# The last row's layernorm, router and slots inside the second layer; its shared expert behind the experts; value sums on VectorE, the keys' maxima through TensorE

## The chip, the cores and the metric

One Trainium2 chip, one of its cores. The metric is device time of one execution in microseconds, and for a kernel the median of its runs. TensorE, VectorE (DVE), ScalarE (ACT), GpSimd (POOL) and the sync engine (SP, which issues most DMAs) each run a stream of instructions of their own, in the order of that stream, and wait for one another by semaphores.

## The reference

Two layers over x of 4 rows x 1024 tokens x 128 channels, in float32. Each layer normalises x and adds two branches of it to x.

```python
xn = _layernorm(x)
x = x + _L0_attn_ref(xn, ...) + _L0_ffn_ref(xn, ...)
xn = _layernorm(x)
x = x + _L1_attn_ref(xn, ...) + _L1_ffn_ref(xn, ...)
```

The first layer is an attention with 16 heads of 8 channels that share keys and values, beside an attention with 8 heads whose values and outputs go through 2 of 8 experts. The second layer, where the change lies, is this, much shortened:

```python
# L1 attention: positive random features, H=16 heads, J=64 features
dash = einsum('bhnd,hjd->bhnj', d**-0.25 * data, proj)
diag = sum(data * data) * 0.5 * d**-0.5
stab_q = max(dash, axis=-1); stab_k = max(dash, axis=(-1, -2))   # per head, over all tokens
feat = J**-0.5 * exp(dash - diag - stab) + EPS_FEAT
out = q' (k'^T v) / max(q' . sum(k'), EPS_DEN)
# L1 ffn: top 2 of 8 experts, and one shared expert for every token
top_w, top_i = top_k(xn @ gate_w + gate_b, 2); gw = softmax(top_w)
out = sum_e combine[:, e] * (gelu(xn @ w1[e] + b1[e]) @ w2[e] + b2[e])
shared = gelu(xn @ ws1 + bs1) @ ws2 + bs2
```

So the keys of a row need the greatest feature of each head over all 1024 tokens, and the constant EPS_FEAT needs the sum of the values over all tokens.

## The kernel before

x stays in SBUF, 128 tokens on the partitions, 8 tiles a row. The first layer is one long loop over units (row, head) with the other attention paced into it. When a row is complete, mqa_out (the last step of its attention) runs layernorm(1, b), which leaves the transposed row xnT[b] by TensorE, and router(b): the logits, the two best experts, by two products with constant matrices (L300) the place of each token in its expert's list, the shares, and at_slot. slot_rows(b) is then a generator of 16 steps; each normalises a tile of 128 tokens on GpSimd (L333), adds token number and share, and scatters it with an indirect DMA into sorted_x in HBM (L340). For rows 0 to 2 that lies within the first layer. Row 3 is complete only with the first layer's last product, so its norm and router stand at the layer's end, before the second layer.

The second layer begins with the loads of its weights (L1185 to L1225) into a pool fw, whose memory is that of the first layer's pools: the first of these is pre (gates and slots), the second wst (weights). Then the tables of blocks (L1236 to L1280): from how many tokens each expert has, which expert and which 256 slots each of 39 blocks takes (block, read by SP) and its bias (b1s).

Two orders are written by hand here, those of TensorE and SP; VectorE's and ScalarE's are planned ahead by the compiler from estimated times. GpSimd's instructions stand in the trace in the order of the program. The order comes from generators, of which each `yield` ends a step:

- favor_keys(b), 19 steps: project keys (kp), project values (v1p, va), diagonals (dg), project queries (qp), the sums of the values (vsum, L1363: 2 x 8 products with a column of ones), then four rounds of features (ddk, L1303): VectorE takes each token's maximum (mk, L1377) and subtracts it (L1313), ScalarE takes the exponential. Then mx is the maximum over the tiles, GpSimd's partition_all_reduce (L1386) makes of it stab, the maximum over all tokens, and VectorE scales va by exp(mk - dg - stab). Three steps later come the products kv (L1408).
- favor_queries(b), 20 steps: ask (ddq and exponentials) four times, turn (qt, 16 transposes) four times, outputs (fo), normalise (ot), turn_back (oT1p) and add (o1w, then x += by VectorE) twice.
- shared(), the shared expert: 8 tiles t of 512 tokens (two a row); ph and Gelu in one step, cT, py and bias in the next, the transposes back (yT) and the addition to x in the one after.
- experts(): for block j load sorted slots and w1, then turn (xgT), load w2, one (pb, Gelu), two (pe, VectorE's scaling yb, and two indirect DMAs with addition into the sums in HBM by GpSimd, L1673).

The fill, shared() and behind it the rest of the slots and experts(), goes between the others by a rate per step: 0.84 beside favor_keys(0) alone, 0.45 beside queries and keys together, 1.2 beside the last queries. In each of these steps the slots of row 3 take one step too. When all is issued, the sums are read back (y, L1738), added to x tile by tile (L1742) and stored (L1744).

The E tiles hold the exponentials, 2048 floats a partition, seven buffers in turn; in layernorm xn lies in cTs tiles, in shared() hT is a tile of its own. all_ones, ident and the PSUM banks (small) are shared by all.

Of the kernel before, what the change touches and what calls it, by code (L numbers as in the profile page):

```python
# [71 lines left out]
def two_layers(ctx: ExitStack, tc: tile.TileContext, a: dict, out: bass.AP):  # L72
# [141 lines left out]
    def layernorm(layer, b, pool):  # L214
# [12 lines left out]
        for q in range(NT // 4):  # L227
            xn = pool.tile([P, 512], F32, tag="cTs", name=f"xn{layer}_{b}_{q}", bufs=3)
# [119 lines left out]
    with ExitStack() as l0:  # L348
        pre = l0.enter_context(tc.tile_pool(name="pre0", bufs=1))
        wst = l0.enter_context(tc.tile_pool(name="wst", bufs=2))  # L350
# [348 lines left out]
        def mqa_out(b):  # L699
# [27 lines left out]

            if b == 0:
                nc.sync.dma_start(gw, a["gate_w"])
                nc.sync.dma_start(gb, a["gate_b"].unsqueeze(0).to_broadcast([P, ME]))  # L730
            while b not in complete:
                yield
# [498 lines left out]
    def brief(k, n, m, name):  # L1231
# [4 lines left out]
    nb = late([P, ME], "nb")  # L1236
    nc.vector.tensor_tensor(nb, filled, begin, ALU.subtract)
    nc.vector.tensor_scalar(nb, nb, 1.0 / MB, None, ALU.mult)
    more = brief(0, ME, PER, "more")
    nc.vector.tensor_tensor(  # L1240
        more, bcast(nb, PER), num[:, 0:PER].unsqueeze(1).to_broadcast([P, ME, PER]), ALU.is_gt
    )
    nc.vector.tensor_reduce(nb, more, axis=AX.X, op=ALU.add)
    upto = late([P, ME], "upto")
    nc.vector.tensor_copy(upto, nb)
    for e in range(1, ME):
        nc.vector.tensor_tensor(
            upto[:, e : e + 1], upto[:, e : e + 1], upto[:, e - 1 : e], ALU.add
        )

    past = brief(0, NBLK, ME, "past")
    full = [P, NBLK, ME]
    nc.vector.tensor_tensor(
        past, bcast(num[:, 0:NBLK], ME), upto.unsqueeze(1).to_broadcast(full), ALU.is_ge
    )
    of = late([P, 2, NBLK], "of")
    nc.vector.tensor_reduce(of[:, 0, :], past, axis=AX.X, op=ALU.add)
    nc.vector.tensor_tensor(past, past, nb.unsqueeze(1).to_broadcast(full), ALU.mult)
    nc.vector.tensor_reduce(of[:, 1, :], past, axis=AX.X, op=ALU.add)
    nc.vector.tensor_tensor(of[:, 1, :], num[:, 0:NBLK], of[:, 1, :], ALU.subtract)  # L1260
    nc.vector.scalar_tensor_tensor(
        of[:, 1, :], of[:, 0, :], float(PER), of[:, 1, :], ALU.mult, ALU.add
    )
    nc.vector.tensor_scalar(of[:, 1, :], of[:, 1, :], float(ME * PER), None, ALU.min)
    nc.vector.tensor_scalar(of[:, 0, :], of[:, 0, :], float(ME - 1), None, ALU.min)
    block = fw.tile([P, 2, NBLK], I32, tag="block", name="block")
    nc.vector.tensor_copy(block, of)

    b1s = late([P, NBLK, MHC], "b1s")
    isit = brief(0, NBLK, ME, "isit")  # L1270
    b1t = brief(1, NBLK, ME, "b1t")
    full = [P, NBLK, ME]
    nc.vector.tensor_tensor(
        isit, bcast(of[:, 0, :], ME), num[:, 0:ME].unsqueeze(1).to_broadcast(full), ALU.is_equal
    )
    for c in range(MHC):
        nc.vector.tensor_tensor(
            b1t, isit, b1[:, 0:ME, c].unsqueeze(1).to_broadcast(full), ALU.mult
        )
        nc.vector.tensor_reduce(b1s[:, :, c], b1t, axis=AX.X, op=ALU.add)  # L1280
# [41 lines left out]
    def favor_keys(b):  # L1322
# [6 lines left out]
        for q in range(2):  # L1329
# [7 lines left out]
            for c in range(2):  # L1337
                for r in range(2):
                    nc.vector.tensor_tensor(
                        va[:, ts(q, 4), c, :, 9 * r : 9 * r + HD], pv[:, :, :, c, r, :],  # L1340
                        bv[:, :, c, r, :].unsqueeze(1).to_broadcast([P, 4, 4, HD]), ALU.add,
                    )
        yield
# [17 lines left out]
        for c in range(2):  # L1361
            for n in range(NT):
                nc.tensor.matmul(  # L1363
                    vsum[:, c : c + 1], lhsT=va[:, n, c].rearrange("p s d -> p (s d)"),
                    rhs=ones[:, 0:1], start=(n == 0), stop=(n == NT - 1),
                )
# [7 lines left out]
        for r in range(NT // 2):  # L1374
# [10 lines left out]
        stab = fa.tile([P, 4, 4], F32, tag="stab", name=f"stab{b}")  # L1385
        nc.gpsimd.partition_all_reduce(  # L1386
            stab.rearrange("p s h -> p (s h)"), mx.rearrange("p s h -> p (s h)"), P,
            bass_isa.ReduceOp.max,
        )
        nc.vector.tensor_tensor(mk, mk, dg[:, 0], ALU.subtract)  # L1390
        nc.vector.tensor_tensor(
            mk, mk, stab.unsqueeze(1).to_broadcast([P, NT, 4, 4]), ALU.subtract
# [7 lines left out]
        yield  # L1400
# [162 lines left out]
    def shared():  # L1563
# [31 lines left out]
        for t in range(B * T // TC + 1):  # L1595
            if t < B * T // TC:
                b, q = divmod(t, T // TC)
                hT = hTs[t] = ff.tile([P, MHC, TC], F32, tag="hT", name=f"hT{t}", bufs=1)
# [7 lines left out]
            if t > 0:  # L1606
                third(t - 1)
            yield
            if t < B * T // TC:
# [93 lines left out]

    def fill():
        yield from shared()
        for it in to_slots.values():
            for _ in it:
                pass
        yield from experts()

    filler = fill()
    due = 0.0
    for k, (rows_now, rate) in enumerate((
        ((0,), 0.84), ((0, 1), 0.45), ((1, 2), 0.45), ((2, 3), 0.45), ((3,), 1.2),
# [3 lines left out]
        for _ in run(*its):  # L1718
            for it in to_slots.values():
                next(it, None)  # L1720
# [85 lines left out]
```

## Time and profile before

| what | us |
|---|---|
| median of 3 runs (lowest, highest) | 3413.81 (3403.72, 3414.24) |
| the profiled execution | 3414.98 |
| its span, first to last instruction | 3413.2 |
| TensorE busy, of the span | 3194.2 (94%) |
| VectorE, ScalarE, GpSimd busy | 2436.3, 1809.7, 1865.8 |
| granted TensorE clock, mean | 0.964 |
| last products of the first layer start | 2887.68 |
| first product of the second layer's own (kp) | 2912.60 |
| first product of the experts (xgT) | 3027.74 |
| last product | 3380.6 |

A line of the timeline gives start and length in us, engine, line and operation, what it writes and reads, how many are merged, and in brackets how long the engine stood before it and what ended that. TensorE's records of one kind follow each other faster than each lasts, since they are pipelined: the distance of their starts is what one costs. A float32 product has two records. A line of the waits gives who waited for whom, us in total, times, and the longest. "issue" in place of a releaser is time in which the profile shows nothing waited for. The granted clock is a share of full speed.

### The profile page before, as it was taken

The page shows a single profiled execution, that of the slowest core. Times are in us where ns is not written, and L with a number is a line of the kernel's source. Part 1 is how long each engine was busy: PE and PEld are TensorE (multiplying, and loading weights), DVE is VectorE, ACT ScalarE, POOL GpSimd, SP SyncE. Part 2 cuts the span into 40 slices and gives each one's busy share as a digit, 9 for nine tenths or more (in the row PEclk, how much of TensorE's full clock was granted, in tenths as well). Part 3 has the DMA queues.
Part 4 walks back from the last instruction along what each step waited for, and adds up shares of the span by engine and source line. Part 5 has one row for each costly group of instructions (what it writes and reads, how often), then busy time and mean ns, then how long its engine had stood idle before and what let it go on. Part 6 is the DMA issues. An engine that isn't in the chain of part 4 may idle for free. (4 is left out here: it accounts for less than half of the span.)

```text
span 3413.2 us, 48756 instructions
## 1 busy us (share of the span) xinstructions
PE 3194.2 (94%) x15386; PEld 1742.3 (51%) x15386; DVE 2436.3 (71%) x4714; ACT 1809.7 (53%) x3157; POOL 1865.8 (55%) x2355
## 2 busy tenths in 40 slices
PE   5899999999999999999999999999999998998996
PEld 2344444555545444554454445455455554567775
DVE  7998686766777867676877876777666645556774
ACT  2234555556555555655455555565566564345663
POOL 1345355666656666665467667656766553313334
PEclk8999999999999999999999999999999999888998
DMA  4122443432323223323232233232323220023346
GB/s 134 52 64 84 126 132 105 118 104 86 93 73 99 72 77 90 96 89 89 62 91 84 83 93 94 89 92 84 96 88 88 79 65 8 19 51 75 79 89 149
DMA packets 449335, 293.67 MB, mean 86 GB/s; under 512 B 41450, under 2 KB 422260, under 8 KB 449076
## 3 DMA queue, kind: packets, MB, share of 16 engines
q1 hardware_dynamic: 404884, 221.32, 23.0%
q0 software_dynamic: 41952, 68.16, 7.3%
q8 instruction: 123, 2.02, 0.2%
q14 instruction: 136, 1.11, 0.1%
q10 hardware_dynamic: 2240, 1.07, 0.1%
HBM read 176.29 MB, written 113.71 MB: 85 GB/s over the span
## 5 line engine op out<-in xcount | busy, mean ns | idle before, releaser
L618 DVE TENSOR_REDUCE nmh<-mx 128x1 f32<-128x512 f32 x1024 | 664.8, 682 | 278.0 <-PE mx L612 276.4
L860 POOL DMA_INDIRECT sorted_v<-xv,gates x448 | 446.7, 997 | 395.0 <-DMA sorted_v<-xv,gates 329.9
L673 ACT ACTIVATE pT<-sT 128x512 f32<-128x512 f32 x1024 | 557.2, 600 | 166.6 <-PE sT L666 97.7
L936 PE MATMUL ss<-xnT,qTs 128*128 128x512 f32 x1024 | 495.8, 606 | 7.2 <-DVE g_o L993 2.6
L941 DVE TENSOR_REDUCE nms<-ps 128x1 f32<-128x1024 f32 x256 | 311.1, 1215 | 256.0 <-ACT ps L939 254.9
L968 PE MATMUL cp<-pTs,vs 128*128 128x512 f32 x1024 | 460.9, 603 | 19.7 <-DVE pTs L960 16.5
L989 PE MATMUL po<-ow,cTs 128*128 128x512 f32 x1024 | 474.3, 595 | 0.7 <-ACT cTs L973 0.7
L821 POOL TENSOR_TENSOR g_o<-g_o 128x256 f32<-128x256 f32 x256 | 192.0, 750 | 465.2 <-DVE g_o L820 434.1
L939 ACT COPY ps<-ss 128x512 f32<-128x512 f32 x512 | 299.9, 587 | 256.1 <-PE ss L936 253.5
L943 ACT ACTIVATE ps<-ps,nms 128x1024 f32<-128x1024 f32 x256 | 294.4, 1150 | 156.1 <-DVE nms L941 155.2
L993 DVE TENSOR_TENSOR g_o<-po,go 128x512 f32<-128x512 f32 x512 | 334.2, 684 | 48.9 <-POOL x L999 26.9
L612 PE MATMUL mx<-ks,qs 72*128 72x512 bf16 x1024 | 312.3, 382 | 12.2 <-DVE nmh L618 5.1
L666 PE MATMUL sT<-qs,ks 75*128 75x512 bf16 x1024 | 310.3, 383 | 13.2 <-DVE nmh L618 9.3
L968 PEld LDWEIGHTS cp<-pTs,vs 128*128 128x128 f32 x1024 | 193.1, 194 | 246.1 <-issue 231.0
L936 PEld LDWEIGHTS ss<-xnT,qTs 128*128 128x128 f32 x1024 | 191.1, 193 | 188.9 <-issue 107.2
L956 PE MATMUL pTp<-ident,ps 128*128 128x128 f32 x2048 | 272.1, 276 | 13.9 <-ACT ps L943 10.4
L956 PEld LDWEIGHTS pTp<-ident,ps 128*128 128x128 f32 x2048 | 241.2, 142 | 81.2 <-issue 16.1
L989 PEld LDWEIGHTS po<-ow,cTs 128*128 128x128 f32 x1024 | 179.4, 191 | 159.1 <-issue 127.1
L973 ACT COPY cTs<-cp 128x512 f32<-128x512 f32 x64 | 37.5, 586 | 411.7 <-PE cp L968 411.7
L912 POOL DMA_INDIRECT vs<-yv,gates x224 | 219.0, 978 | 67.2 <-issue 56.6
L912 POOL DMA_INDIRECT yg<-yv,gates x224 | 217.6, 972 | 68.3 <-issue 68.0
L1673 POOL DMA_INDIRECT sum<-yb,whose x78 | 123.9, 1588 | 235.3 <-DVE yb L1669 199.1
(308 smaller groups left out, 4992.9 us busy)
## 6 DMA issues: line engine op xcount, KB each, us to landing
vb<-in_v_w_dram SPq DMA_DIRECT2D x644, 64.0 KB
xs<-sorted_v SPq DMA_DIRECT2D x140, 256.0 KB
yv<-xs SPq DMA_DIRECT2D x140, 256.0 KB
w<-in_w_dram SPq DMA_DIRECT2D x78, 256.0 KB
sorted_x<-nobody SPq DMA_DIRECT2D x16, 1040.0 KB
ow<-in_o_w_dram SPq DMA_DIRECT2D x32, 512.0 KB
qs<-qd SPq DMA_DIRECT2D x144, 64.0 KB
sorted_v<-xv,gates POOLq DMA_INDIRECT x448
```

What stands on the lines that cost most here:

```text
L612: nc.tensor.matmul(sc, lhsT=qs[0:NPAIR, i, ts(n, P)], rhs=ks[0:NPAIR, ts(kc, 512)], start=True, stop=True,)
L618: nc.vector.tensor_reduce(halves[:, i, n, kc : kc + 1], sc, axis=AX.X, op=ALU.max)
L666: nc.tensor.matmul(sc, lhsT=ks[:, ts(kt, P)], rhs=qs[:, i, ts(c, 512)], start=True, stop=True,)
L673: nc.scalar.activation(pT, sc, AF.Exp)
L860: nc.gpsimd.indirect_dma_start(out=sorted_v[u % 4][:, :], out_offset=bass.IndirectOffsetOnAxis(ap=column(u, k, n).bitcast(I32), axis=0), i ...
L912: nc.gpsimd.indirect_dma_start(out=to[:, n, :], out_offset=None, in_=unit[u, "y"][:, :], in_offset=bass.IndirectOffsetOnAxis(ap=column(u, ...
L936: nc.tensor.matmul(sc, lhsT=qT[:, ts(n, P)], rhs=xnT[b][:, ts(c, 512)], start=True, stop=True)
L941: nc.vector.tensor_reduce(nm, p, axis=AX.X, op=ALU.max, negate=True)
L956: nc.tensor.transpose(pt[:, ts(k, P)], p[:, ts(4 * k4 + k, P)], ident)
L968: nc.tensor.matmul(cp, lhsT=v[:, kt, :], rhs=pT[:, kt, :], start=(kt == 0), stop=(kt == NT - 1),)
L989: nc.tensor.matmul(po, lhsT=cT[:, ts(qt, P)], rhs=unit[u, "ow"][:, ts(c, 512)], start=True, stop=True,)
L993: nc.vector.tensor_tensor(g[:, ts(c, 4), :], po.rearrange("p (e c) -> p e c", e=4), bcast(go[:, ts(c, 4)], P), ALU.mult,)
```

## The change

1. mqa_out no longer norms and routes row 3. A generator last_row does it inside the second layer: layernorm with xn in E tiles, router, the tables of blocks (now the generator tables, same instructions), then the row's 16 slots. It takes two steps after each step of the loop.
2. shared() takes a range of tiles. Tiles 0 to 5 come first, then the experts, then tiles 6 and 7, which are row 3's, with hT in E tiles.
3. The sums of the values over a row's 8 tiles are made by one VectorE reduce into vs; TensorE keeps 2 products of 16.
4. The keys' maxima: mx is transposed by TensorE, reduced by VectorE, set on a diagonal (each) and sent to all partitions by a product with all_ones. favor_keys has 20 steps.
5. The rates beside queries and keys are 0.5 in place of 0.45; the first layer's pools wst and pre change places.

```diff
     with ExitStack() as l0:
+        wst = l0.enter_context(tc.tile_pool(name="wst", bufs=2))
         pre = l0.enter_context(tc.tile_pool(name="pre0", bufs=1))
-        wst = l0.enter_context(tc.tile_pool(name="wst", bufs=2))
...
+            if b == B - 1:
+                return
             while b not in complete:
                 yield
             yield from layernorm(1, b, sw)
...
+    def wide(name):
+        t = fa.tile([P, 2, 4, 4, FJ], F32, tag="E", name=name, bufs=7)
+        return t.rearrange("p a b c d -> p (a b c d)")
+
+    def last_row():
+
+        yield from layernorm(1, B - 1, ff, lambda name: wide(name)[:, 0:512])
+        yield from router(B - 1)
+        yield from tables()
+        yield
+        yield from to_slots[B - 1]
...
+        vs = fa.tile([P, 2, 4, 32], F32, tag="vs1", name=f"vs1_{b}")
+        nc.vector.tensor_reduce(
+            vs, va.rearrange("p n c s d -> p c s d n"), axis=AX.X, op=ALU.add
+        )
         yield
...
         for c in range(2):
-            for n in range(NT):
-                nc.tensor.matmul(
-                    vsum[:, c : c + 1], lhsT=va[:, n, c].rearrange("p s d -> p (s d)"),
-                    rhs=ones[:, 0:1], start=(n == 0), stop=(n == NT - 1),
-                )
+            nc.tensor.matmul(
+                vsum[:, c : c + 1], lhsT=vs[:, c].rearrange("p s d -> p (s d)"),
+                rhs=ones[:, 0:1], start=True, stop=True,
+            )
...
-        stab = fa.tile([P, 4, 4], F32, tag="stab", name=f"stab{b}")
-        nc.gpsimd.partition_all_reduce(
-            stab.rearrange("p s h -> p (s h)"), mx.rearrange("p s h -> p (s h)"), P,
-            bass_isa.ReduceOp.max,
+        nc.vector.tensor_tensor(mk, mk, dg[:, 0], ALU.subtract)
+        yield
+
+        pt = small(f"mxT{b}")
+        nc.tensor.transpose(pt[0:NH, 0:P], mx.rearrange("p s h -> p (s h)"), ident)
+        top = fa.tile([NH, 1], F32, tag="top", name=f"top{b}")
+        nc.vector.tensor_reduce(top, pt[0:NH, 0:P], axis=AX.X, op=ALU.max)
+        each = fa.tile([NH, NH], F32, tag="each", name=f"each{b}")
+        nc.vector.tensor_scalar(each, ident[0:NH, 0:NH], top, None, ALU.mult)
+        yield
+        stab = small(f"stab{b}")
+        nc.tensor.matmul(
+            stab[:, 0:NH], lhsT=all_ones[0:NH, :], rhs=each, start=True, stop=True
         )
...
-        yield
         yield
         yield
...
+                hT = wide(f"hT{t}").rearrange("p (c n) -> p c n", c=MHC) if first_t else \
+                    ff.tile([P, MHC, TC], F32, tag="hT", name=f"hT{t}", bufs=1)
...
+    SOON = 3 * T // TC
+    aside = last_row()
+
     def fill():
-        yield from shared()
-        for it in to_slots.values():
-            for _ in it:
-                pass
+
+        yield from shared(0, SOON)
+        for _ in aside:
+            pass
         yield from experts()
+        yield from shared(SOON, B * T // TC)
...
-        ((0,), 0.84), ((0, 1), 0.45), ((1, 2), 0.45), ((2, 3), 0.45), ((3,), 1.2),
+        ((0,), 0.84), ((0, 1), 0.5), ((1, 2), 0.5), ((2, 3), 0.5), ((3,), 1.2),
...
         for _ in run(*its):
-            for it in to_slots.values():
-                next(it, None)
+            next(aside, None)
+            next(aside, None)
             due += rate
```

## The prediction

> **What bounds the kernel now.** I read the busy line of the page first (TensorE 94%), then a table of stretches cut at the borders of the second layer's loop, then the waits of the sync queue and of all engines after 2895 us, and last the timelines of TensorE, GpSimd and the end. The columns below are: stretch, length, busy time and count of PE, PEld, DVE, ACT, POOL, granted clock, DMA share, GB/s.
>
> ```profile
> core 0: us, PE busy (x) PEld busy (x) DVE busy (x) ACT busy (x) POOL busy (x), PEclk, DMA share, GB/s
> 2896.00:2912.60 16.60, 6.29 (x28) 5.79 (x29) 9.97 (x41) 5.53 (x7) 3.04 (x6) 0.54 0.21 51
> 2912.60:3001.50 88.90, 85.87 (x341) 45.45 (x341) 48.10 (x121) 36.67 (x45) 36.51 (x67) 0.91 0.04 13
> ...
> 3121.00:3215.50 94.50, 87.00 (x718) 69.98 (x716) 71.68 (x157) 57.75 (x72) 31.36 (x28) 0.93 0.36 76
> 3215.50:3308.30 92.80, 86.50 (x707) 70.90 (x706) 69.97 (x152) 54.89 (x70) 29.50 (x27) 0.89 0.35 74
> 3308.30:3380.60 72.30, 71.28 (x553) 62.19 (x552) 45.38 (x103) 44.09 (x74) 43.37 (x39) 1.00 0.61 123
> 3380.60:3413.20 32.60, 0.00 (x1) 0.00 (x0) 11.69 (x18) 0.00 (x0) 5.96 (x4) 0.57 0.79 203
> ```
>
> TensorE sets the second layer, but not evenly: 10 us lie idle before its first product, its last 32.6 us hold none, and the clock of 0.9 in the middle says that stalls stretch what looks busy.
>
> ```profile
> 2902.81 2.18 PE L239 MATMUL lnT<-ident,xn 128*128 128x128 f32 x8 [7.99 <-DVE xn L232]
> 2904.78 3.44 PE L283 MATMUL router<-gw,xnT 128*128 128x8 f32 x16
> 2911.72 0.66 PE L300 MATMUL before<-mask,before_me 128*128 128x64 f32 x2 [3.50 <-DVE mask L296]
> ...
> 2987.74 3.70 PE L1601 MATMUL ph<-xnT,ws 128*128 128x512 f32 x8
> ...
> 2997.46 3.70 PE L1601 MATMUL ph<-xnT,ws 128*128 128x512 f32 x8
> ...
> 3027.74 0.66 PE L1636 MATMUL xgT<-ident,xg 128*128 128x128 f32 x4
> ```
>
> The last row's norm and router stand alone on TensorE; the two ph rows give 9.72 us for one tile of the shared expert; the experts begin at 3027.74.
>
> ```profile
> 2966.38 1.09 POOL L340 DMA_INDIRECT sorted_x<-xslot,at_slot  x1 [0.98 <-DMA sorted_x<-xslot,at_slot]
> 2987.21 0.40 POOL L1386 PARTITION_ALL_REDUCE stab<-mx  x1 [19.75 <-issue]
> 2994.35 0.81 POOL L333 TENSOR_SCALAR xslot<-x,mv,rstd 128x128 f32<-128x128 f32 x1 [6.74 <-issue]
> ```
>
> GpSimd scattered 13 of the row's 16 slot tiles from 2926.80 to 2966.38 (39.58/12 = 3.3 us each), stood until the keys' maxima came, and after the reduce stood 6.74 more.
>
> ```profile
> SPq L1621 <- DMA sorted_x<-xslot,at_slot: 71.2, 1, 71.2
> ```
>
> ```profile
> DVE sv L1368 <- PE vsum L1363: 17.3, 4, 5.3
> ...
> DVE mk L1391 <- POOL stab L1386: 9.8, 4, 5.7
> PE kv L1408 <- DVE va L1398: 9.3, 2, 8.1
> ```
>
> The experts' first load waits for the last scatter (to 3005), yet TensorE asks for it only 22 us later: the scatter chain is hidden now, and the change takes away what hides it. The three waits are those of the value sums and of the maxima.
>
> **The change, part by part.** All sums are against the profiled execution (3414.98 us, span 3413.2, so 1.8 around it), which is 1.2 above the median of 3413.81.
>
> *The row moves inside: when the experts can start.* TensorE's last product of layer one starts at 2887.68 and runs 7.13, so kp can start at 2896 instead of 2912.6. It needs Wk1T; the load now waits for the last reader of gates and goes at 2894.90. With the pools swapped it lies on early freed tiles; if that gains nothing, kp comes 2 us later. TensorE's order up to the router's second product (pc), by start-to-start times where the clock was full: kp 1.8, v1p 1.85, ph 3.54, dg 1.7, qp 1.8, lnT twice 1.0, the tile's second half (cT, py) 5.66, ph and yT 4.07, dg 1.7, vsum 0.2, router 1.85, second half 5.66, ddk 1.07: 33. Add 2.7 for the slow start (kp 3.52, v1p 2.57 at 2912) and 2 for waits on cT copies: pc at 2896 + 37.7 = 2934 (2912 now), done 0.9 later. From pc to at_slot it takes 12.8 now, with other VectorE work between; alone its rows add to 4.5. I take 9, because eight feature instructions of 0.6 each share VectorE there: 2944. Sixteen slots, no reduce among them: 16 x 3.3 = 53, to 2997. Then as now 1.7 to the load's issue and 2.3 to landing: first turn at about 3001 (2989 with no slow start and 4.5; 3006 with 12.8).
>
> TensorE gets there sooner: keys 14, row 4.7, six shared tiles 58.3 (6 x 9.72), waits 7.5: 2896 + 84.5 = 2980. So a **new wait of about 20 us** stands in front of the first turn, and kv of row 0 is behind it. Still 27 us earlier than 3027.74. All the row's DMAs are counted: the 16 scatters; SP's loads for block 0 stand behind them as now. The tables of blocks (small VectorE rows, from 2920.9 to 2943 now, other work between) end before the scatters do; that covers them.
>
> *From the first turn to the experts' last product.* Now 3027.74 to 3380.6: 352.9. The fill counts by the code (19 steps of keys, 20 of queries: 0.84 x 19, 0.45 x 39 three times, 1.2 x 20 = 92.6 of 95 fill steps, which the four products left at the end confirm) become 0.84 x 20, 0.5 x 40 three times and 1.2 x 20; the 91st step, the last expert, falls on step 12 of the last query pass. So its steps 13 to 20 come after: tb0 0.44, fo 1.85, o1w 0.9, ot 0.87, tb1 0.44, o1w 0.9 = -5.4. vsum of rows 1 to 3 cost 4.43 + 3.57 + 5.67 = 13.7 start to start; two of 32 products stay: -12.8. kv, kvt, ddq twice, kp and v1p (3.5 + 0.3 + 2.1 + 1.8 + 1.9) were done before 3027.74 and now follow: +9.6. Transpose and broadcast product of the maxima: 4 records of some 0.12 a row, 3 rows: +1.5. kv's 9.3 us of waits go; the new chain crosses TensorE twice with one or two fill steps between and may wait for DVE: I keep 3, so -6 (bounds -9.3 and +9.3). Sum 339.8; last expert product at 3001 + 340 = 3341.
>
> VectorE pays for the sums: 8 x 256 elements a row. The contiguous rows (512 in 682 ns, 1024 in 1215) extrapolate to 2.3 us; the strided reduce of 128 elements (368 ns, against 276 for the contiguous one of 128) puts 3.7. I take 3.0, which lies beside TensorE's projections, where VectorE waited 17.3 us for vsum; where that cover is gone it costs 3 a row. The SBUF page of the Trainium skill (SBUF — State Buffer, under Door 1: The DMA port swizzle) speaks against this edit: each access that crosses to a new 16-byte line pays. This read steps 1,024 bytes; the two rows agree in direction, and by the worse one the four rows cost 5.5 us more of VectorE than by the contiguous one.
>
> The maxima leave GpSimd, where one reduce ran 0.39 to 0.90 us but twice came with a gap of 6.7. The GPSIMD Engine Reference (4.1 Engine selection) gives reductions along partitions to GpSimd. By that rule the -6 would be 0 and the sum 6 higher; the two gaps are why I side with the row.
>
> Tiles in E's buffers instead of cTs and hT cost nothing: seven buffers turn, and each new tile's predecessor was read long before; a missed one would cost a step, some 3 us.
>
> *The end.* Behind the last expert product TensorE has the 5.4 of queries and two shared tiles, 19.5, and about 2 of waits on copies by ScalarE (yT behind acc, o1w behind oT): +27. Then x += o1w 0.69 and 0.2, two y adds 1.5, and the last store (3408.5 to 3413.2) 4.7: +34.
>
> ```profile
> 3386.54 1.55 POOL L1673 DMA_INDIRECT sum<-yb,whose  x1 [0.30 <-issue]
> 3387.91 15.15 SPq L1738 DMA_DIRECT2D y<-sum  x16
> ```
>
> The other branch is the one that ends the kernel now: last product, 7.3 to the first y load, 25.3 to the end: +32.6. The two are nearly level; the shared tiles lie wholly beside the transfers. End: 3341 + 34 = 3375 of span, 38 less than 3413.2. Profiled 3377, beside the median **3376**.
>
> **The rivals.**
> 1. *The wait is filled.* If at_slot comes by 2938, or if the denser fill goes into stalls of the middle passes (their work at full clock is about 73 of 93 us, so 20 each are lost), 12 to 24 us more go: about 3358. For it: clock 0.89 to 0.93 there. Against: fill does not help where VectorE is late.
> 2. *VectorE becomes the bound.* It is busy 70 to 72 of 93 in those passes. If freed TensorE time turns into waits, the -12.8 falls and 3 x 1.7 stays of the sums, about +17: 3393. Against: vsum sat where VectorE idled.
> 3. *The hidden end is not hidden.* VectorE's order is planned; with a y add ahead of the cT copy, the second shared tile starts after the transfers and adds 10 to 20: 3391; with 2 together, 3405, about no change.
> 4. *Slower: the slot chain slips.* The row crosses between VectorE and TensorE five times (xn, xnT, lg, mask, pc). Where an order written for one engine and planned for the other misses, a crossing waits for a step of keys with its fill on TensorE, about 6, and a round of features on VectorE, 4.8: 10.8. Each moves the scatters and the first turn by as much. The gain of 38 is used up when at_slot comes after 2982, at four misses; all five give 3375 + 54 = 3429. For it: today's 12.8 us from pc to at_slot hold a 3.0 us wait of VectorE for an unrelated dg. Against: each crossing has about 6 us of fill to be ready in, and its own work is 1 to 4.
>
> **How the numbers follow.** About 0.3%, 10 us, is what a measurement of this kernel can tell from no change. Forecast 0.45; rival 1 0.20; rival 2 0.17; rival 3 0.11, a third of it as no change; rival 4 0.07, half of it slower. Faster comes to 0.88, less 0.02 for the far edge of rival 2: 0.86; same 0.09; slower 0.05. The range holds the forecast with its bounds (first turn -12 to +5, maxima up to +15), rival 1 and rival 2: 3350 to 3401; above it lie rival 4 and half of 3.
>
> **What would show it.** Right: kp near 2897; no reduce on GpSimd; 16 scatters in about 53 us without a break; the load of block 0 ends TensorE's wait at about 3001; vsum as two products a row; last expert product near 3341, ph and py between it and the end, y loads under them. Wrong: at_slot after 2955, or no wait at the first turn; passes longer than 95 us; TensorE idle for ten us among the last shared products.

## The result and the profile after

The changed kernel takes 3363.92 us (median of four runs, 3353.22 to 3366.61) beside 3412.85 for the kernel before (four runs, 3403.72 to 3414.24): a ratio of 0.985, 95% interval 0.983 to 0.9869, some 49 us less. The forecast was 3376 and the range 3350 to 3401.

The profiled execution of the changed kernel took 3353.22 us, the lowest of its four, with a span of 3351.2. That is 62 us under the profiled execution of before, and the first thing to see is that not all of it belongs to the change. Up to the end of the first layer both kernels issue the same instructions in the same order on TensorE, ScalarE and GpSimd, and on VectorE too but for a few among its last 21, yet the last product of that layer ended at 2894.8 us in the profile of before and at 2875.9 here. Over the thirteen profiles of this study (two kernels and eleven experiments) that point lies between 2875.9 and 2894.8, mean 2888.5. It goes with the time for which the granted clock stood at half during the first layer: 99.0 us in this profile, 122.9 in that of before (correlation over the thirteen 0.81). So every time below is counted from that point, called **E** here, and the thirteen profiles can be compared without that noise.

| us after E | before | forecast | after |
|---|---|---|---|
| first product of the second layer (kp) | 17.8 | 1.2 | 2.0 |
| router's second product (pc) | 16.9 | 39.2 | 41.1 |
| scatters of row 3, first to last start | 32.0 to 107.4 | 49 to 99 | 56.7 to 107.0 |
| first product of the experts (xgT) | 132.9 | 106 | 111.9 |
| last product of the experts | 485.8 | 446 | 441.2 |
| last product of TensorE | 485.8 | 473 | 468.3 |
| end | 518.4 | 480 | 475.3 |

The second layer became 43 us shorter, where 38 were forecast. This way of reading adds up: the mean of E and the 1.8 us around the span, added to the stage's 475.3, give 3365.6, within 2 us of the median of four. For before they give 3408.7, and 4 us of its median stay unassigned.

The busy line of the page after:

```profile
PE 3161.5 (94%) x15286; PEld 1712.1 (51%) x15286; DVE 2450.3 (73%) x4726; ACT 1817.6 (54%) x3164; POOL 1865.9 (56%) x2351
```

TensorE is busy 33 us less (3194.2 before), VectorE 14 more (2436.3 before). The value sums went from one to the other: by their groups TensorE is spared 17.6 us of products (19.9 before, 2.3 now). Of TensorE's 33 us, 11 lie ahead of E, where its instructions are the same. The next view is the table of stretches of the kernel after, cut at its own borders (kp to the experts' first product, three middle passes, the last pass up to the experts' last product, the rest). Columns: stretch, length, busy time and count of PE, PEld, DVE, ACT and POOL, granted clock, DMA share, GB/s.

```profile
2877.90:2987.80 109.90, 86.52 (x336) 44.63 (x336) 62.10 (x164) 46.73 (x53) 40.32 (x71) 0.84 0.07 19
3002.00:3091.70 89.70, 83.75 (x718) 67.86 (x717) 75.56 (x162) 59.80 (x77) 34.77 (x30) 0.96 0.42 89
3091.70:3183.00 91.30, 84.37 (x723) 67.71 (x721) 76.07 (x163) 59.91 (x77) 34.70 (x30) 0.96 0.41 88
3183.00:3272.70 89.70, 83.75 (x719) 67.82 (x718) 75.72 (x161) 59.81 (x77) 34.54 (x30) 0.96 0.43 89
3272.70:3316.90 44.20, 43.18 (x350) 37.20 (x350) 35.34 (x76) 33.26 (x48) 23.93 (x21) 1.00 0.48 94
3316.90:3351.20 34.30, 25.86 (x110) 13.16 (x108) 17.23 (x33) 7.84 (x12) 5.28 (x4) 0.87 0.77 192
```

Three things stand in it. The middle passes took 90 to 91 us where the second and third had taken 94.5 and 92.8, and their clock is 0.96 where it was 0.93 and 0.89. They hold as many product records as before or more, although 28 records of value sums have left each of them: that is the denser fill. The first middle pass of before had taken 106 us:

```profile
3015.00:3121.00 106.00, 91.32 (x709) 72.14 (x708) 72.67 (x156) 58.80 (x75) 22.09 (x20) 0.86 0.27 61
```

The last 34.3 us, which had held no product, hold 25.9 us of TensorE. And the first row of the table is bad: 23.4 of 109.9 us idle, and a clock of 0.84.

That first stretch on TensorE, by its timeline (start, length, engine, line, what it writes and reads, and in brackets the idle time ahead and what ended it):

```profile
2917.00 0.44 PE L301 MATMUL before<-mask,before_me 128*128 128x64 f32 x2
...
2946.62 2.07 PE L1614 MATMUL py<-cTs,bias 10*128 10x512 f32 x2 [5.62 <-DVE cTs L1607]
...
2987.78 0.66 PE L1670 MATMUL xgT<-ident,xg 128*128 128x128 f32 x2 [12.01 <-DMA xg<-sorted_x]
2990.17 0.69 PE L1670 MATMUL xgT<-ident,xg 128*128 128x128 f32 x2 [1.73 <-DMA xg<-sorted_x]
```

The new wait at the experts' first turn is there, 13.7 us of it (12.01 and 1.73), and the shared tiles, too, had to wait for copies by VectorE, 8.3 us in all up to the turn. The sync queue's waits in the same stretch show who holds the load:

```profile
SPq L1655 <- DMA sorted_x<-xslot,at_slot: 48.5, 1, 48.5
```

GpSimd's timeline shows the scatters themselves, the first and the last of the sixteen:

```profile
2932.58 1.10 POOL L341 DMA_INDIRECT sorted_x<-xslot,at_slot  x1 [0.28 <-POOL xslot L340]
...
2982.88 1.09 POOL L341 DMA_INDIRECT sorted_x<-xslot,at_slot  x1 [0.97 <-DMA sorted_x<-xslot,at_slot]
```

That is 50.3 us from first to last start, 3.35 each, with no break. In before the reduce and its two gaps lay among them, 75.4 us in all.

### The profile page after: what moved, and what is told of

Read it like the earlier page. It is cut to its first block, busy times and chain, and to the rows that moved or that the text cites. A ratio compares the mean times of both kernels' runs of the same rounds, so it can differ in the third digit from the quotient of the medians.

```text
span 3351.2 us, 48567 instructions
## 1 busy us (share of the span) xinstructions
PE 3161.5 (94%) x15286; PEld 1712.1 (51%) x15286; DVE 2450.3 (73%) x4726; ACT 1817.6 (54%) x3164; POOL 1865.9 (56%) x2351
## 5 line engine op out<-in xcount | busy, mean ns | idle before, releaser
L997 DVE TENSOR_TENSOR g_o<-po,go 128x512 f32<-128x512 f32 x512 | 334.0, 683 | 44.3 <-POOL x L1003 21.9
L960 PEld LDWEIGHTS pTp<-ident,ps 128*128 128x128 f32 x2048 | 243.2, 143 | 81.4 <-issue 17.4
L657 PE MATMUL ov<-pT,va 128*32 128x512 f32 x2048 | 248.4, 603 | 0.0
```

Source lines behind the costliest of these rows:

```text
L960: nc.tensor.transpose(pt[:, ts(k, P)], p[:, ts(4 * k4 + k, P)], ident)
L997: nc.vector.tensor_tensor(g[:, ts(c, 4), :], po.rearrange("p (e c) -> p e c", e=4), bcast(go[:, ts(c, 4)], P), ALU.mult,)
```

## The experiments

The theory under test is the prediction's own: the gain is made of an earlier first turn (part 1 and, through GpSimd, part 4), the end hidden (part 2), fewer products (part 3) and kv waits gone (part 4). The rivals: the pools or the first layer gave it; the denser fill gave it by going into stalls; part 1 gives nothing. Ten kernels differ from one of the two by one thing, or from another experiment by one; the eleventh repeats the change. Medians are of five runs (six for maxima undone, twelve for pools alone), beside the kernel before on the same chip at 3413.17, 3412.86 and 3413.9 in the three sessions. "Stage" is the end of the kernel counted from E in its profile. A stage is one execution and a median five, and E differs between executions, so the two can tell somewhat different sizes; both are given. A stage, too, can differ by some us from one execution to the next: up to the first turn the kernels with the end and with the rate undone issue the same instructions in the same order as the change, a few in the last us aside, and yet their last scatters start 6 and 4 us sooner.

| kernel | median | ratio, 95% | kp | scatters | first turn | turn to last expert product | from there to the end | stage |
|---|---|---|---|---|---|---|---|---|
| change repeated | 3362.07 | 0.9844, 0.9825 to 0.9863 | 2.0 | 56.0 to 106.2 | 111.2 | 329.8 | 33.6 | 474.6 |
| pools alone | 3413.35 | 0.9998, 0.9985 to 1.001 | 17.8 | 30.9 to 107.5 | 133.7 | 354.4 | 32.3 | 520.4 |
| pools undone | 3358.70 | 0.9842, 0.9821 to 0.9864 | 2.0 | 56.5 to 106.8 | 111.6 | 329.6 | 34.0 | 475.2 |
| row undone | 3350.96 | 0.9812, 0.9793 to 0.9832 | 17.8 | 34.2 to 82.6 | 95.0 | 329.4 | 33.5 | 457.9 |
| end undone | 3373.66 | 0.9887, 0.9869 to 0.9904 | 2.0 | 53.2 to 101.4 | 121.3 | 330.1 | 29.6 | 481.0 |
| sums undone | 3373.42 | 0.9885, 0.9868 to 0.9903 | 2.0 | 64.8 to 113.7 | 118.5 | 340.0 | 33.5 | 492.1 |
| maxima undone | 3378.49 | 0.9907, 0.9887 to 0.9927 | 2.0 | 56.6 to 118.1 | 122.9 | 331.5 | 33.6 | 487.9 |
| rate undone | 3383.97 | 0.9911, 0.9893 to 0.9929 | 2.0 | 54.9 to 103.0 | 107.9 | 350.1 | 33.2 | 491.2 |
| row sooner | 3351.38 | 0.9819, 0.9797 to 0.9841 | 2.1 | 42.1 to 91.1 | 101.7 | 329.4 | 33.7 | 464.8 |
| row undone, 0.55 | 3349.97 | 0.9814, 0.9791 to 0.9836 | 17.8 | 34.3 to 82.8 | 95.1 | 316.8 | 44.3 | 456.2 |
| row undone, 0.6 | 3355.51 | 0.9833, 0.9811 to 0.9854 | 17.8 | 34.6 to 84.3 | 99.4 | 303.7 | 61.9 | 465.0 |

**The change repeated**, unedited, on the chip and in the session of the first three experiments:

> The changed kernel itself once more. Its first profiled execution ended the first layer (last po product) 18.9 us earlier than that of the kernel before, with the same instructions in the same order up to there. Theory A (the first layer varies from one execution to the next): this profile shows the last po product anywhere from 2869 to 2888, while the second layer (from there to the end) takes 475 +-5; time 3353 to 3367. Theory B (the exchanged pools make the first layer faster): again 2869 +-4, and a time near 3353.

Measured 3362.07, with a stage of 474.6 beside 475.3 in the first profile, while E was 2892.0 beside 2875.9. So in these two profiles the second layer is the same to a microsecond, and the 16 us between the two profiles are the first layer's.

**The pools.** Once the exchange of wst and pre alone in the kernel before, once undone in the changed one.

```diff
     with ExitStack() as l0:
-        pre = l0.enter_context(tc.tile_pool(name="pre0", bufs=1))
         wst = l0.enter_context(tc.tile_pool(name="wst", bufs=2))
+        pre = l0.enter_context(tc.tile_pool(name="pre0", bufs=1))
```

> The kernel before with nothing but the first layer's pools wst and pre exchanged. Theory A: the same time within 0.2% (3406 to 3420), since kp waits for the last row's router, not for its weights; only the weights' loads go out earlier, before 2880. Theory B (the addresses speed up the first layer): 6 to 19 us less, ratio 0.994 to 0.998, all of it ahead of the last po product.

> The changed kernel with the pools in their old order. The prediction put this part at up to 2 us: the loads of the second layer's weights wait for the last reader of gates, some 7 us before the first layer's end, and bd, ws1 and the rest come one after the other, so that kp starts 2 us later and the chain to the experts' first turn with it: 0 to +5. Rival: the later loads of bd and ws stop TensorE's early steps, 8 to 15 us. Theory B: +6 to +19, all in the first layer.

Alone it does nothing that can be measured (ratio 0.9998), and undone in the changed kernel it leaves kp at E + 2.0 and the stage at 475.2. The earlier kp comes from the row's move alone.

**The row undone.** Row 3 is normed and routed at the end of the first layer again, with the tables ahead of the loop; the slots take one step per step of the loop as before. Parts 2 to 5 stay.

```diff
-            if b == B - 1:
-                return
             while b not in complete:
...
-        yield from layernorm(1, B - 1, ff, lambda name: wide(name)[:, 0:512])
-        yield from router(B - 1)
-        yield from tables()
-        yield
         yield from to_slots[B - 1]
+    for _ in tables():
+        pass
...
             next(aside, None)
-            next(aside, None)
```

> The changed kernel with part 1 alone undone: the last row is normed and routed ahead of the second layer and the tables of blocks are made there; its slots take one step after each step from the first on. Theory (the slot chain and TensorE's fill trade places): kp starts 16 us later, but the scatters start 25 us earlier, are done at +83 to +90 after the first layer's end, and TensorE reaches the first turn without a wait at about +111 instead of +100 with a wait until +112. So the time changes by less than 4 us: the earlier start is eaten by the new wait. Rival (the earlier start is the gain): 12 to 16 us slower.

Measured 3350.96 (3346.61 to 3353.66) beside 3362.07 (3359.51 to 3368.63) for the change in the same session: no run of the one reaches the other (of the four runs in the result above one does, 3353.22, the one with the earliest E). Undoing the part that gave the change its first words makes the kernel 11 us **faster** by the medians, 17 by the stage. The expectation, a difference under 4 us, and the rival, a slower kernel, both missed. The first stretch of this kernel (kp to the experts' first turn) beside the 109.90 above:

```profile
2906.70:2983.90 77.20, 73.56 (x309) 37.34 (x310) 50.52 (x120) 34.63 (x41) 38.93 (x70) 0.98 0.12 35
```

and TensorE at its end:

```profile
2983.38 0.66 PE L1620 MATMUL yT<-ident,acc 128*128 128x128 f32 x4 [0.60 <-ACT acc L1613]
2983.87 0.60 PE L1667 MATMUL xgT<-ident,xg 128*128 128x128 f32 x4
```

The stretch is 32.7 us shorter, the start 15.8 later, so the turn comes 17 sooner. Only 3.6 us of it are idle, the clock is 0.98, and xgT follows the shared tile without a wait, since the scatters ended 24 us sooner (E + 82.6 beside 107.0). Inside the layer the row's chain costs TensorE 20 us more of idle time, 13.7 of them at the turn, and 13 more of busy time, part of which is the row's own products and part the same products at a lower clock.

**The row sooner.** Is it the row's place inside the layer, or that it is taken too slowly? Three steps of last_row per step of the loop in place of two, everything else as changed.

```diff
             next(aside, None)
             next(aside, None)
+            next(aside, None)
             due += rate
```

> The changed kernel with three steps of the last row after each step of the loop in place of two, nothing else. Undoing part 1 alone made the kernel 13 us faster; this run asks by which way part 1 loses. Theory (the row's chain through TensorE's hand-written order is late: the router's second product stands behind two shared tiles and at +41 after the first layer's end, its slots begin at +57 and end at +107): with three steps that product comes one shared tile and two steps of keys earlier, near +27 and ahead of the first features on VectorE, slots from +36 to +87, the first turn without a wait at +95 to +100, and the time 11 to 16 us below the changed kernel (3347 to 3352). Rival (the row's own work and the tables inside the second layer cost the time, wherever they stand): first turn at +108 or later, within 4 us of the changed kernel.

Measured 3351.38, as the theory had it: about the row undone. pc comes at E + 34.3 (41.1 in the change, 27 expected), the scatters end at 91.1 (107.0), the turn comes without a wait at 101.7 (111.9). So most of the loss is the lateness of the chain in TensorE's hand-written order, 10.5 of 17.4 us by the stage, and 7 us of the stage remain against the row undone. The waits of TensorE from E to the first turn in this kernel (who, for whom, total, times, longest) show what the speed costs:

```profile
PE lnT L240 <- DVE xn L233: 6.8, 2, 3.5
PE lnT L240 <- issue: 3.7, 1, 3.7
```

With fewer fill products between them, the row's own crossings are waited for, 10.5 us on TensorE. The median of 3351.38 lies within 0.5 us of the row undone, though the stage of the profiled execution is 7 longer; which of the two is the better kernel these runs can't tell.

**The end undone.** All eight shared tiles before the experts.

```diff
-    SOON = 3 * T // TC
+    SOON = B * T // TC
```

> The changed kernel with all eight shared tiles ahead of the experts, none behind. Theory: 19.5 us of products come ahead of the first turn, where TensorE now waits 13.7 us, so the first turn is 6 to 8 later; the last expert product comes at step 16 of the last query pass instead of 12, 4 to 5 more; the end keeps its 32.6 of transfers instead of 34. Together 9 to 12 us slower. Rival (the two tiles behind the experts are worth their whole 19.5 us): 18 to 21 us slower.

Measured 3373.66, 11.6 over the change, within the 9 to 12 expected; by the stage it is only 6. The first turn comes 9.4 us later, since two tiles lie in front of it again; what lies behind the last expert product is 4.5 shorter (29.6). The two tiles cost 19 us of TensorE, but ahead of the turn they fill the new wait: in this trace the load of block 0 is not waited for.

**The sums undone.** TensorE sums the values with 16 products a row again.

```diff
-        vs = fa.tile([P, 2, 4, 32], F32, tag="vs1", name=f"vs1_{b}")
-        nc.vector.tensor_reduce(
-            vs, va.rearrange("p n c s d -> p c s d n"), axis=AX.X, op=ALU.add
-        )
         yield
...
-            nc.tensor.matmul(
-                vsum[:, c : c + 1], lhsT=vs[:, c].rearrange("p s d -> p (s d)"),
-                rhs=ones[:, 0:1], start=True, stop=True,
-            )
+            for n in range(NT):
+                nc.tensor.matmul(
+                    vsum[:, c : c + 1], lhsT=va[:, n, c].rearrange("p s d -> p (s d)"),
+                    rhs=ones[:, 0:1], start=(n == 0), stop=(n == NT - 1),
+                )
```

> The changed kernel with the value sums on TensorE, 16 products a row, and no reduce by VectorE. Theory (TensorE sets the middle passes): rows 1 to 3 cost 12.8 us again; row 0's 4 to 5 fall before the wait at the first turn and cost 0 to 4 by a later router: 11 to 17 us slower. Rival (VectorE sets these passes): the reduce it is spared, 2.3 to 3.7 us a row, pays for the products: between 4 us faster and 4 us slower.

Measured 3373.42, 11 over the change, the near end of the theory's 11 to 17 (stage +17, of which 7 before the turn and 10.2 behind it; the profile is that of the slowest of the five runs, 3384.58). Row 0's sums in this kernel by TensorE's timeline, which stand ahead of the router's second product:

```profile
2921.16 6.17 PE L1383 MATMUL vsum<-ones,va 128*128 128x1 f32 x32
```

The same tile by the timeline of the kernel after:

```profile
2904.95 0.59 PE L1386 MATMUL vsum<-ones,vs 128*128 128x1 f32 x4
```

For row 0 the saving is 5.6 us of the 8.1 by which pc comes later without the edit (E + 49.2 against 41.1), and the scatters follow pc. VectorE's group in the kernel after (busy, mean ns, idle before) has its price:

```profile
L1364 DVE TENSOR_REDUCE vs<-va 128x256 f32<-128x2048 f32 x4 | 14.7, 3669 | 0.0
```

It is 3.67 us each, the strided bound of the prediction (3.7) and not the 3.0 taken. The Trainium skill's rule that reads across 16-byte lines pay (SBUF — State Buffer, Door 1: The DMA port swizzle) pointed the right way; the contiguous rows extrapolated to 2.3. The edit gains all the same: TensorE is spared 17.6 us of products, and the 14.7 that VectorE pays lie beside TensorE's work.

**The maxima undone.** GpSimd reduces the keys' maxima in the step of mx; the steps stay.

```diff
+        nc.gpsimd.partition_all_reduce(
+            stab.rearrange("p s h -> p (s h)"), mx.rearrange("p s h -> p (s h)"), P,
+            bass_isa.ReduceOp.max,
+        )
         nc.vector.tensor_tensor(mk, mk, dg[:, 0], ALU.subtract)
         yield
...
-        nc.tensor.transpose(pt[0:NH, 0:P], mx.rearrange("p s h -> p (s h)"), ident)
-        nc.vector.tensor_reduce(top, pt[0:NH, 0:P], axis=AX.X, op=ALU.max)
-        nc.vector.tensor_scalar(each, ident[0:NH, 0:NH], top, None, ALU.mult)
...
-            stab[:, 0:NH], lhsT=all_ones[0:NH, :], rhs=each, start=True, stop=True
```

> The changed kernel with GpSimd's reduce for the keys' maxima, issued in the step of mx; the steps and the fill are those of the changed kernel. Theory: row 0's reduce stands between the row's slots in GpSimd's order and brings its gap of some 6.7 us back, so the first turn is 6 to 13 us later; rows 1 to 3 wait 0 to 8 us more before kv. Together 6 to 18 us slower. Rival (the maxima were hidden, only the steps between them and kv count): within 3 us, and the scatters keep 3.2 us each without a break.

Measured 3378.49, 16 over the change (stage +13), within the 6 to 18 of the theory. GpSimd's timeline of this kernel, around row 0's reduce:

```profile
2982.70 1.09 POOL L341 DMA_INDIRECT sorted_x<-xslot,at_slot  x1 [1.01 <-DMA sorted_x<-xslot,at_slot]
2989.90 0.39 POOL L1409 PARTITION_ALL_REDUCE stab<-mx  x1 [6.11 <-issue]
2997.18 0.81 POOL L334 TENSOR_SCALAR xslot<-x,mv,rstd 128x128 f32<-128x128 f32 x1 [6.88 <-issue]
```

A reduce of 0.39 us stands in 13 us of idle GpSimd. The trace by source line names what begins each gap, on the sequencer of GpSimd (POOLq; count, duration in ns, first and last start):

```profile
L1409 POOLq MODIFY_POOL_CONFIG  x4: 32/318/610, 2984.1 to 3105.9; - x4
L334 POOLq MODIFY_POOL_CONFIG  x2: 88/88/88, 2990.3 to 2990.3; - x2
```

Two such instructions stand at 2984.1, right behind the end of a scatter and 5.8 us ahead of the reduce, and two at 2990.3, on the line of the slots and 6.9 us ahead of the next slot. Row 1's reduce has two as well (3105.9), and 6.59 us of idle GpSimd. The reduces of rows 2 and 3 have none, and no idle time. The kernel before has the same pairs at the same places, ahead of its gaps of 6.74 and 6.78 us; the changed kernel has none beyond the first microsecond of the program. So the gaps come with MODIFY_POOL_CONFIG; what the engine does in them, no run shows.

The scatters behind the reduce end at E + 118.1 in place of 107.0. That is 11 of the 13 us of the stage. From turn to last expert product the edit is worth the remaining 2 (331.5 against 329.3 and 329.8), though that is where the prediction had its gain, in the kv waits. TensorE's wait for va ahead of kv, 9.3 us before, is gone in the changed kernel; in this one, which keeps the added step, this much is left:

```profile
PE kv L1433 <- DVE va L1424: 3.8, 1, 3.8
```

How much of the waits the added step removed, and how much the way of the maxima, no run separates.

**The rate undone.** 0.45 in the three middle passes.

```diff
-        ((0,), 0.84), ((0, 1), 0.5), ((1, 2), 0.5), ((2, 3), 0.5), ((3,), 1.2),
+        ((0,), 0.84), ((0, 1), 0.45), ((1, 2), 0.45), ((2, 3), 0.45), ((3,), 1.2),
```

> The changed kernel with the rates beside queries and keys at 0.45 again. The stretch from the first turn to the last expert product came out 11 us shorter than the prediction summed. Theory (the denser fill goes into stalls of the middle passes): the last expert product moves to step 17 of the last query pass and that stretch grows by 8 to 14 us; the time by 5 to 12, since the queries' rest behind it shrinks by 4. Rival (TensorE's work is the same, only its order differs): that stretch grows by the 4 to 5 us of query products that now come ahead of its end, and the time stays within 3 us.

Measured 3383.97, 22 over the change (stage +16.6): more than the 5 to 12 of the theory, and far from the rival. The three middle passes, to be read beside the three of the change in the first table:

```profile
3012.40:3104.40 92.00, 80.66 (x695) 63.94 (x694) 74.73 (x159) 55.83 (x71) 31.66 (x27) 0.94 0.38 80
3104.40:3197.20 92.80, 83.07 (x696) 66.44 (x695) 75.01 (x160) 55.94 (x71) 31.46 (x27) 0.91 0.37 78
3197.20:3289.00 91.80, 82.76 (x695) 65.58 (x694) 74.70 (x158) 55.98 (x71) 31.37 (x27) 0.93 0.37 79
```

With 23 to 27 fewer product records in each, the passes are 1.5 to 2.3 us *longer*. TensorE stands idle 9 to 11 us of each, against 6 to 7 in the change, and the granted clock is lower, 0.91 to 0.94 against 0.96. More fill in these passes costs no time up to 0.5, and what was not filled here lies behind, where TensorE is busy nearly without a gap. The rate alone is worth 20 us of this stretch (350.1 against 329.8). Some 5 of these are query products that change sides of the last expert product, as the prediction counted them: 21.5 us of TensorE lie behind it here, 27.1 in the change. Apart from the fill, the instructions of the three passes stand in nearly the same order in both kernels on TensorE, VectorE and ScalarE (15 of 393 places differ on VectorE), so it is the fill that makes the difference. The turn came 3 to 4 us sooner here with the same instructions ahead of it; that is not the rate's.

**How far does that go?** The row undone, with 0.55 and with 0.6.

```diff
-        ((0,), 0.84), ((0, 1), 0.5), ((1, 2), 0.5), ((2, 3), 0.5), ((3,), 1.2),
+        ((0,), 0.84), ((0, 1), 0.55), ((1, 2), 0.55), ((2, 3), 0.55), ((3,), 1.2),
```

> The kernel with part 1 undone, and rates of 0.55 in place of 0.5 beside queries and keys. The three middle passes took 92 to 93 us at 0.45 and 90 to 91 at 0.5: the extra 4.5 us of expert products in each cost nothing. Theory (these passes are set by the chain through VectorE, and fill is free until TensorE's work, 75 us a pass at 0.5, nears 91): passes of 90 to 93 again, the last expert product at step 7 of the last query pass, 14 to 18 us earlier, the end 8 to 11 us earlier, since more queries are left behind it: 3340 to 3344. Rival (0.5 is where TensorE fills up): passes of 94 to 96, and the time within 3 us of 3351.

> As the one before with rates of 0.6. Theory: TensorE's work is 82 us a pass, passes of 91 to 95, last expert product near the start of the last query pass, and the end set by TensorE's products behind it alone: 8 to 18 us below 3351. Rival: passes of 98 or more and no gain over 0.5.

Measured 3349.97 and 3355.51, against 3350.96 with 0.5: both theories missed, no time is gained. The passes now take 91.7 to 95.0 and 95.3 to 95.6 us. At 0.6 the second of them is this:

```profile
3090.60:3185.80 95.20, 89.09 (x770) 72.76 (x769) 77.46 (x169) 60.49 (x83) 41.40 (x36) 1.00 0.47 101
```

The clock is full there, so more products now make the pass longer. The last expert product does come 12 and 21 us sooner, but what is left of the last query pass then stands bare behind it. Two lines of TensorE's timeline near the end of the 0.6 kernel:

```profile
3326.93 3.31 PE L1488 MATMUL qt<-ident,qE 128*128 128x128 f32 x16 [2.80 <-ACT qE L1331]
...
3337.59 1.08 PE L1542 MATMUL oT1p<-ident,o 128*128 128x128 f32 x4 [2.77 <-DVE o L1532]
```

It waits for ScalarE and VectorE between these steps with no fill to put there, so TensorE ends at E + 456.8 in place of 450.7. Of the rates run, 0.5 and 0.55 are the best; 0.6 is 5 us behind by the median, with runs that overlap, and 7 by the stage. The three fastest kernels, row undone with 0.5 and 0.55 and row sooner, lie at 3350 to 3351, 11 to 14 us under the change, and cannot be told apart.

**Not tried:** more buffers for the slots, to shorten the 3.35 us of a scatter. In the trace each scatter's idle time ends with the one before it (the bracket in the line above), and in the program each writes the same tensor as the one before; that more buffers would change nothing is argued from this, not shown.

## Why the prediction was right, and where it was not

The time fell in the range and on the right side, 12 us under the forecast. About 6 of these are the first layer: the sums were made against a profile whose E of 2894.8 is the latest of thirteen. The other 5 are the second layer (475 against 480), and there two misses of 6 and -10 offset each other: that the sum came so near is in part luck. Two of its own figures are a little off: the slow start's rows give 2.4 us and not 2.7, and by its own terms the first turn's bounds are about -7 and +4, not -12 and +5. Neither moves the forecast.

1. **Start of the second layer.** Forecast E + 1.2, measured 2.0. The 2 us that the prediction gave to the pools were nothing, as the two pool runs show.
2. **pc.** Forecast +39.2, measured 41.1. From kp to pc that is 39.1 where the sum said 38, so the sum of start-to-start times held.
3. **From pc to at_slot.** Forecast 9, measured 13.3, as long as the 12.8 of before: VectorE interleaves features there. The choice between the two bounds was wrong; the row of before was the better guide than the chain alone.
4. **Sixteen slots.** Forecast 53, measured 51.4 to the end of the last scatter, with no break.
5. **The new wait.** Forecast about 20, measured 13.7. Its end came 6 late (steps 2 and 3) and TensorE got there 15 late (+99.9 against 85). The step that failed is TensorE's arrival: its products were summed at full clock, 77 us, and took 86.5 at a granted clock of 0.88 up to the wait; its idle time on the way was 11.4 us where 7.5 were allowed, 8.3 of it for the copies of cT.
6. **Turn to last expert product.** Forecast 339.8, measured 329.3. Right in the terms: some 5 of queries moved, the sums' products gone (forecast 12.8, by the sums undone 10 to 11). The step that failed is the one that left the passes' own length alone. The prediction counted the denser fill as products to be moved, at no change of what stalls; the rate undone shows that fill in those stalls costs no time, and goes with a higher clock. That is the second half of rival 1, given 0.20. The rate is 20 us of this stretch by itself, some 15 of them beyond the 5.4 that the prediction counted.
7. **The maxima.** The forecast of -6 put the gain on the kv waits. These did go (9.3 us to none), but with the added step kept the edit is worth only 2 there; 11 us come from the two gaps around GpSimd's reduce, ahead of the last scatters, which the prediction had seen in part (6.74 behind the reduce) and counted only in "no reduce among them". The size was off and so was the place.
8. **VectorE's sums.** Taken at 3.0, measured 3.67 each; rival 2 (VectorE the bound) did not come, since it is busy 76 of 90 us in passes that grew shorter.
9. **The end.** Forecast 34, measured 34.1. Both branches were nearly level, as forecast: with the shared tiles gone from there it is 29.6.

The sign of the whole was right, but the largest part by its words was not: moving the row in costs 11 us (medians) and the others pay for it. Rival 4, the slot chain that slips, is what happened in small: pc at 41.1 instead of 16.9 makes the scatters end at 107.0 where, with GpSimd freed of the reduce, they would have ended at 82.6. The prediction compared its first turn with the turn of before, 132.9, and so gave the move a gain that the other parts make without it: with the row undone the turn comes at 95.0. By undoing one part at a time the stage loses 6 (end), 17 (sums), 13 (maxima), 16 (rate), 0 (pools) and gains 17 (row). These add to 35 and not to 43. The parts that bring the scatters forward share one wait and so need not add up, but with stages that differ by some 4 us between executions the gap of 8 shows little.

Open: what GpSimd does in the gaps that begin with MODIFY_POOL_CONFIG; why E varies by 19 us beyond its correlation with the half clock; how much of what the denser fill gains is the clock and how much the stalls themselves; and some 4 us of before's median.

## What to carry to other kernels

Price each part of a change against the kernel with the other parts already in it: the row's move looked like 16 us won at the first product, and was 11 lost in a kernel whose other parts had already brought the first turn forward. Before moving a chain that ends in a long serial piece (here sixteen scatters of 3.35 us), ask when that piece starts, not when the engine that feeds it becomes free. Where a pass is set by waits between engines, put in more independent work until its length begins to grow (here between 0.5 and 0.55 fill steps per step of the loop), and count from a fixed point of the program when executions differ ahead of it.

## What the hardware showed that was not expected

- Fuller passes had a higher granted clock and were shorter: 0.96 and 90 to 91 us with 718 to 723 product records, 0.91 to 0.94 and 92 to 93 us with 695. With 770 the clock was 1.00, but the pass 95.2 us. That stalls pull the clock down is the reading that fits. The Trainium skill says the like of short idle times between groups of products (TensorE: Matmul & The Clock Gate, Part 1, on a second failure mode, in another kernel); no run here tested what sets the clock.
- The same first layer took 2875.9 to 2894.8 us over thirteen executions, with 99 us at half clock in the shortest and 122.9 in the longest. The same page (Part 1, What's actually happening) says that a kernel's slow start varies from run to run and is under 1% of a typical span. The spread here, 19 us or 0.65% of the layer, is not larger, but it gathers over the whole layer and exceeds what most of these edits moved.
- One partition_all_reduce of 0.39 us between scatters came with 6.11 us of idle GpSimd ahead of it and 6.88 behind, each begun by two MODIFY_POOL_CONFIG on the sequencer. In this trace and that of before, 5.8 to 7.1 us passed from such a pair to GpSimd's next instruction wherever that one waited for nothing else (five pairs), on the way to the reduce and, in row 0, on the way back; two reduces a kernel came without a pair and without a gap. The same maximum by transpose, VectorE reduce and a product with ones took 2.9 us in row 1, from the start of the transpose mxT (3075.61) to that of the product stab (3078.47), other work between.
